# A cross-attention kernel: a new order for its first slots and its end, and output weights loaded one chunk per slot

## The chip, the cores and the metric

The kernel runs on one NeuronCore of a Trainium2 chip. The metric is the device time of one execution in microseconds (us). TensorE is written PE in the profile (its weight loads PEld), VectorE is DVE, ScalarE is ACT, GpSimd is POOL and SyncE, which issues all the DMA transfers of this kernel, is SP.

## What is computed

The input x has 32 batches of 512 rows and 640 columns; the context has 32 batches of 77 rows and 1024 columns. There are 20 heads of 32 columns. Cut to what the kernel computes (the reference also slices a further 24 context rows, but the context it is given ends after 77, so those parts are empty):

```python
q = heads(x @ to_q_w)                     # (32, 20, 512, 32)
k = heads(ctx @ to_k_w)                   # (32, 20, 77, 32)
v = heads(ctx @ to_v_w)
p = softmax(q @ k.T / sqrt(32))           # over the 77 keys
out = merge(p @ v) @ to_out_w + to_out_b + x
```

Everything is float32. To keep that precision on PE, each operand is split into a high part (a rounded copy, made by ACT) and a low part (the remainder, a subtraction on DVE or POOL), and a product is three matmuls: high by high, high by low, low by high.

## The kernel before

A first stage, up to about 284 us in the profile, turns the context into keys and values for all batches, which go to scratch memory in DRAM, splits the weights, and prepares the first batch of x. The main stage then runs 160 *slots*. Slot n works on batch b = n // 5 and on the group j = n % 5 of four heads (128 of the 640 columns). The order of the instructions on every engine is the order in which the program text emits them (the schedule is written out by hand), so each engine, SP's DMA queue included, is a queue in program order that stops at the first instruction whose inputs are not ready.

A slot holds several stages of different slots' work:

- `scores(n, t)` for the four row blocks t = 0 to 3 of slot n: three matmuls (L381) into one of three PSUM banks named sc, then a maximum on DVE (L389). `exps(n, t)` follows on ACT: four exponentials with their row sums (L399).
- `queries(n + 1, ...)`: fifteen matmuls (L346) for the next slot's queries, and `split_q(n + 1)`: three ACT copies (L357, L361) and two DVE subtractions (L363).
- `normalize(n - 1)`: reciprocal of the sums on DVE (`sums`, L409), then one large multiplication on POOL (L414). `transpose_p(n - 1)`: one DVE transpose (L421) of the normalized probabilities into the one buffer z, then four DMAs to a DRAM scratch pd (L428).
- `load_p(n - 2)`: two DMAs (L437, L438) that bring the transposed probabilities of slot n - 2 back as raw.
- for the slot three back, m = n - 3 (called *taken*, from slot 3 on): `cast_p` (ACT, L445), `rest_p` (ACT, L451, and DVE, L452), and `last_p` (POOL, L459) split raw into high and low parts pp. `values(m)` are eight matmuls (L473): the first needs only `cast_p`, the second also the subtraction of `rest_p`, and the last two also L451 and `last_p`. `split_a(m)` (L104 on ACT, L105 on DVE) splits the result into at.
- from slot 7 on, two *output pieces* of twelve matmuls each (`piece`, `project`, L503), which multiply at by the output weights wo_s for a batch that is complete; slots 0 to 6 have none (`has_out` is false). `finish` adds a finished half row block to the residual (DVE, L531) and, after the second half, sends the 128 x 640 block out (SP, L535). `load_residual` (L492) and `add_bias` (POOL, L496) prepare the residual.
- beside these, single steps for coming batches: loads of keys and values (`refill`, L323, L326, L333), of x (`load_x`, L226), and its transposes and splits (L230, L237, L238).

In slots 0 and 1, values of the last group of the context are computed as well (`context_values`, L200, 24 matmuls a call). From slot 2 on, the output weights come back from DRAM in five chunks of 640 KB (L731): two after slot 2, two after slot 3, one after slot 4.

After slot 159, `end()` drains the pipeline: it holds the probabilities of slots 157, 158 and 159, the last pieces (6 to 9) of batch 30, and all eight half row blocks of batch 31. Those are opened by `begin` with the heads that are ready and closed with the last group of heads, j = 4, after `take(N - 1)`, which is `values` and `split_a` of slot 159.

Within a slot PE's program order is: scores 0, two fifths of the queries, scores 1, the rest of the queries, scores 2, first piece, values of the slot three back, scores 3, second piece. On POOL it is: normalization of slot n - 1, low part of slot n - 3, then bias and splits. On DVE the transpose of slot n - 1 stands ahead of the query subtractions of slot n + 1.

Of the kernel before, what the change touches and what calls it, by code (L numbers as in the profile page):

```python
# [23 lines left out]
P = 128  # L24
# [26 lines left out]
def kernel(  # L51
# [25 lines left out]
    nc = tc.nc  # L77
    B, S, C = x.shape
    CA = ehs.shape[2]
    NT = B * NKEY  # L80
    NQ = S // P
    NC_ = C // P
# [3 lines left out]
    N = B * NC_  # L86
# [307 lines left out]
    def exps(n, t, sc, nm):  # L394
        if t == 0:
            sms[n] = main.tile([P, NQ * HPC], F32, tag="sm", name="sm", bufs=2)
        for i in range(HPC):
            at = t * HPC + i
            nc.scalar.activation(  # L399
                pnb[n % 2][:, at, :NKEY],  # L400
                sc[:, i * NKEY : (i + 1) * NKEY],
                AF.Exp,
                bias=nm[:, i : i + 1],
                accum_out=sms[n][:, at : at + 1],
            )

    def sums(n):
        rs = main.tile([P, NQ * HPC], F32, tag="rs", name="rs", bufs=2)
        nc.vector.reciprocal(rs, sms.pop(n))  # L409
        return rs  # L410

    def normalize(n, rs):
        pf = pnb[n % 2][:, :, :NKEY]
        nc.gpsimd.tensor_tensor(  # L414
            pf, pf, rs.unsqueeze(2).to_broadcast([P, NQ * HPC, NKEY]), ALU.mult
        )
# [31 lines left out]
    def rest_p(n):  # L448

        raw, pp = raws[n], pps[n]  # L450
        nc.scalar.copy(pp[:64, 4, :], raw[:64, 2, :])  # L451
        nc.vector.tensor_tensor(  # L452
            pp[:, 2:4, :], raw[:, 0:2, :], pp[:, 0:2, :].bitcast(F32), ALU.subtract
        )
# [62 lines left out]
    def piece(b, i):  # L517
        for t, h, j in STEPS[4 * i : 4 * i + 4]:
            if j == 0:
                output_bank(b, t, h)  # L520
            project(b, t, h, j)
            if j == NC_ - 1:
                closed.append((b, t, h))

    def finish():

        while closed:
            b, t, h = closed.pop(0)
            xr = xrs[b, t]
            cols = slice(h * HALF, (h + 1) * HALF)  # L530
            nc.vector.tensor_tensor(  # L531
                xr[:, cols], pos.pop((b, t, h))[:, :HALF], xr[:, cols], ALU.add
            )
            if h == 1:
                nc.sync.dma_start(out[b, t * P : (t + 1) * P, :], xr)  # L535

    LATE = 2
# [13 lines left out]
    def take(m):  # L551
        values(m)
        split_a(m)
# [14 lines left out]
    def slot(n, beside=()):  # L568
        b, j = divmod(n, NC_)
        ahead, more = n + 1 < N, b + 1 < B  # L570
        back, first = PIECES[j]
        bo_, has_out = b - back, b >= back
        xsplits = SPLIT_X.get(j, ((), ())) if more and n > LATE else ((), ())
        turns = TRANSPOSE_X.get(j, ((), (), ())) if more and b else ((), (), ())
        taken = takes.get(n)

        refill(b, j, 0)
        if taken is not None:
            cast_p(taken)
        s = scores(n, 0)  # L580
        if taken is not None:
            rest_p(taken)
        if n:
            normalize(n - 1, sums(n - 1))
        if taken is not None:
            last_p(taken)
        exps(n, 0, *s)
        if ahead:
            queries(n + 1, 0, 2)
        s = scores(n, 1)  # L590
        if n - LAG + 1 in pds and n > LATE:
            load_p(n - LAG + 1)
        refill(b, j, 1)
        finish()
        if j == 4 and b + 2 < B:
            load_x(b + 2, (0, 1))
        if j in RESIDUAL and b >= RESIDUAL[j][0]:
            load_residual(b - RESIDUAL[j][0], RESIDUAL[j][1])
        if j in BIAS and b >= BIAS[j][0]:
            add_bias(b - BIAS[j][0], BIAS[j][1])  # L600
        exps(n, 1, *s)
        for i in turns[0]:
            transpose_x(b + 1, i)
        if ahead:
            queries(n + 1, 2, NC_)
        s = scores(n, 2)
        if n:
            transpose_p(n - 1)
        if ahead:
            split_q(n + 1)  # L610
        exps(n, 2, *s)
        if j == 4 and b + 2 < B:
            load_x(b + 2, (2, 3))
        for c in xsplits[0]:
            split_x(b + 1, c)
        if has_out:
            piece(bo_, first)
        if taken is not None:
            values(taken)
        if len(beside) > 0:  # L620
            context_values(*beside[0], psv)
        s = scores(n, 3)
        finish()
        for i in turns[1]:
            transpose_x(b + 1, i)
        if taken is not None:
            split_a(taken)
        for c in xsplits[1]:
            split_x(b + 1, c)
        exps(n, 3, *s)  # L630
        if len(beside) > 1:
            context_values(*beside[1], psv)
        if has_out:
            piece(bo_, first + 1)
        for i in turns[2]:
            transpose_x(b + 1, i)

    def end():


        last = B - 1
        load_p(N - 2)
        cast_p(N - 3)
        rest_p(N - 3)
        last_p(N - 3)
        normalize(N - 1, sums(N - 1))
        transpose_p(N - 1)
        finish()
        add_bias(last - 1, 3)
        piece(last - 1, 6)  # L650
        piece(last - 1, 7)
        finish()
        load_p(N - 1)
        load_residual(last, 0)
        load_residual(last, 1)
        piece(last - 1, 8)
        take(N - 3)
        piece(last - 1, 9)
        cast_p(N - 2)
        rest_p(N - 2)  # L660
        last_p(N - 2)
        finish()
        spare = late[0].tile([P, 3, S], F32, tag="raw", name="xr", bufs=2)
        load_residual(last, 3, spare.rearrange("p k q -> p (k q)")[:, :C])
        load_residual(last, 2)

        def begin(i, j0, j1):
            t, h = divmod(i, 2)
            if j0 == 0:
                if i < 3:  # L670
                    pos[last, t, h] = ps.tile([P, S], F32, tag="sc", name="po", bufs=3)
                elif i == 3:
                    pos[last, t, h] = ps.tile([P, S], F32, tag="pq", name="po", bufs=1)
                elif i < 7:
                    output_bank(last, t, h)
                else:
                    pos[last, t, h] = late[1].tile([P, S], F32, tag="pa", name="po", bufs=1)
            for j in range(j0, j1):
                project(last, t, h, j)

        begin(0, 0, 2)
        begin(1, 0, 2)
        take(N - 2)
        cast_p(N - 1)
        rest_p(N - 1)
        last_p(N - 1)
        for t in (0, 1, 3, 2):
            add_bias(last, t)
        begin(2, 0, 3)
        begin(0, 2, 4)  # L690
        begin(1, 2, 4)
        begin(2, 3, 4)
        for i in range(3, 6):
            begin(i, 0, 4)
        take(N - 1)
        begin(6, 0, 4)
        begin(7, 0, 4)
        for t in range(NQ):
            for h in range(2):
                project(last, t, h, 4)  # L700
                closed.append((last, t, h))
            finish()

    with tc.manual_schedule(engines=ENGINES):
        g0, gn = GROUPS_KV[-1]
        load_keys(0, 0)
        halves = [(g0, gn, t0, h) for t0 in range(0, gn, P) for h in range(2)]
        queries(0, 0, NC_)
        split_q(0)
        for half in halves[:2]:  # L710
            context_values(*half, psv)
        for i in range(NQ):
            transpose_x(1, i)
        for c in range(2):
            split_x(1, c)
        for half in halves[2:4]:
            context_values(*half, psv)
        for n in range(LATE):
            slot(n, halves[4 + 2 * n : 6 + 2 * n])
        psv.release()  # L720
        kvp.release()
        late.append(ctx.enter_context(tc.tile_pool(name="late", bufs=1, reuse_waits="tile")))
        late.append(
            ctx.enter_context(tc.tile_pool(name="psl", bufs=1, space=PSUM, reuse_waits="tile"))
        )
        load_p(0)
        wos.append(late[0].tile([P, NC_, 2, C], FPR, name="wo_s"))
        for n in range(LATE, LATE + 4):
            slot(n)
            for k in {LATE: (0, 1), LATE + 1: (2, 3), LATE + 2: (4,)}.get(n, ()):  # L730
                nc.sync.dma_start(wos[0][:, k].bitcast(F32), wo_dram[:, k].bitcast(F32))  # L731
        for n in range(LATE + 4, N):
            slot(n)
        end()


# [38 lines left out]
```

## Time and profile before

| what | us |
|---|---|
| median of 3 runs (lowest to highest) | 1980.47 (1978.42 to 1981.48) |
| the profiled execution | 1980.38 |
| its span in the trace | 1978.6 |
| PE busy with matmuls | 1946.0 |
| ACT busy | 1595.6 |
| DVE busy | 1345.8 |
| POOL busy | 986.0 |

The profiled execution took 1980.38 us, of which the trace covers 1978.6 us from the first to the last event; the other 1.8 us lie around the traced span. "Busy" is the time in which an engine had an instruction running. For PE that does not mean full speed: the PE clock column of the profile gives the share of full speed that the hardware granted in a stretch of time, and a matmul at a lower granted clock is longer and still counts as busy. In the lists below a line gives start, duration, engine, program line, operation, output and inputs, and in brackets the idle time ahead of it with the instruction that ended it. In tables by stretch, each engine has its busy time and, in parentheses, the number of its instructions; the last three columns are the granted PE clock, the mean busy share of the 16 DMA engines and the rate in GB/s.

Most slots look alike. Slot 8, from 373.60 to 383.89 us, has PE busy for all of its 10.29 us, and so does every slot after it until 1933 us.

### The profile page before, as it was taken

The page shows a single profiled execution, that of the slowest core. Times are in us where ns is not written, and L with a number is a line of the kernel's source. Part 1 is how long each engine was busy: PE and PEld are TensorE (multiplying, and loading weights), DVE is VectorE, ACT ScalarE, POOL GpSimd, SP SyncE. Part 2 cuts the span into 40 slices and gives each one's busy share as a digit, 9 for nine tenths or more (in the row PEclk, how much of TensorE's full clock was granted, in tenths as well). Part 3 has the DMA queues.
Part 4 walks back from the last instruction along what each step waited for, and adds up shares of the span by engine and source line. Part 5 has one row for each costly group of instructions (what it writes and reads, how often), then busy time and mean ns, then how long its engine had stood idle before and what let it go on. Part 6 is the DMA issues. An engine that isn't in the chain of part 4 may idle for free.

```text
span 1978.6 us, 38192 instructions
## 1 busy us (share of the span) xinstructions
PE 1946.0 (98%) x11012; PEld 1761.7 (89%) x11012; DVE 1345.8 (68%) x2156; ACT 1595.6 (81%) x6377; POOL 986.0 (50%) x620
## 2 busy tenths in 40 slices
PE   9999998999999999999999999999999999999998
PEld 7889996799999999999999999999999999999997
DVE  4443235777777777777777777777777777777763
ACT  3322137899999999999999999999999999999982
POOL 0000033566555555565555666655665556655644
PEclk9999999899999999999999999999999999999999
DMA  7994368888889898889888988888888888888975
GB/s 170 217 263 120 96 146 206 212 220 228 228 220 229 224 225 230 225 231 225 228 223 225 226 229 221 234 223 228 226 227 226 225 224 219 225 228 225 231 195 156
DMA packets 555996, 423.54 MB, mean 214 GB/s; under 512 B 170191, under 2 KB 459501, under 8 KB 555789
## 3 DMA queue, kind: packets, MB, share of 16 engines
q1 hardware_dynamic: 555789, 421.10, 83.8%
q8 instruction: 91, 1.49, 0.3%
q14 instruction: 116, 0.95, 0.2%
HBM read 245.61 MB, written 175.32 MB: 213 GB/s over the span
## 4 chain that ended last, share of the span: by engine, by line
PE 90%; DMA 4%; SPq 2%; ACT 1%; DVE 1%; issue 1%; POOL 1%; DVEq 0%; ACTq 0%; POOLq 0%
PE po L503 28%; PE pq L346 28%; PE pa L473 15%; PE sc L381 10%; PE pv L200 4%; PE pk L171 4%; DMA raw<-pd 1%; SPq L114 1%; DMA k_dram<-ks 1%; SPq L155 1%; DMA v_dram<-vs 1%; DMA wraw<-in_L_xattn_to_k_w_dram 0%; POOL pn L414 0%; DMA wraw<-in_L_xattn_to_out_w_dram 0%; DMA cs<-in_ctx_dram 0%
## 5 line engine op out<-in xcount | busy, mean ns | idle before, releaser
L399 ACT ACTIVATE pn<-sc,nm 128x77 f32<-128x77 f32 x2560 | 797.6, 328 | 44.6 <-DVE nm L389 31.1
L414 POOL TENSOR_TENSOR pn<-pn,rs 128x1232 f32<-128x1232 f32 x160 | 364.3, 2277 | 670.2 <-DVE rs L409 655.4
L503 PE MATMUL po<-wo_s,at 128*128 128x320 f32 x3840 | 626.9, 312 | 3.0 <-DVE xr L531 3.0
L346 PE MATMUL pq<-xt,wq_s 128*128 128x512 f32 x2400 | 621.0, 399 | 0.0
L503 PEld LDWEIGHTS po<-wo_s,at 128*128 128x128 f32 x3840 | 566.3, 189 | 3.6 <-DVE xr L531 3.2
L399 ACT ACTIVATION_READ_ACCUMULATOR pn<-sc,nm 128x1 f32 x2560 | 529.3, 207 | 0.0
L389 DVE TENSOR_REDUCE nm<-sc 128x4 f32<-128x308 f32 x640 | 294.5, 460 | 335.0 <-PE sc L381 330.6
L346 PEld LDWEIGHTS pq<-xt,wq_s 128*128 128x128 f32 x2400 | 430.4, 190 | 76.7
L473 PE MATMUL pa<-pp,vb 128*128 128x512 f32 x1280 | 331.2, 400 | 13.0 <-POOL pp L459 11.0
L238 POOL TENSOR_TENSOR xt<-xs,xt 128x512 fp32r<-128x512 f32 x160 | 203.9, 1292 | 269.2 <-ACT xt L237 262.0
L473 PEld LDWEIGHTS pa<-pp,vb 128*128 128x128 f32 x1280 | 243.3, 197 | 53.7 <-POOL pp L459 13.5
L421 DVE STREAM_TRANSPOSE z<-pn 128x1280 f32<-128x1280 f32 x160 | 241.0, 1506 | 21.4 <-POOL pn L414 19.7
L452 DVE TENSOR_TENSOR pp<-raw,pp 128x1024 fp32r<-128x1024 f32 x160 | 196.2, 1226 | 59.5 <-ACT pp L445 52.8
L381 PEld LDWEIGHTS sc<-kc,qt 128*128 128x128 f32 x1280 | 213.0, 190 | 23.6 <-issue 2.1
L381 PE MATMUL sc<-kc,qt 128*128 128x154 f32 x1280 | 223.1, 256 | 2.4 <-DVE qt L363 2.3
L459 POOL TENSOR_TENSOR pp<-raw,pp 64x512 fp32r<-64x512 f32 x160 | 208.7, 1305 | 27.0 <-ACT pp L451 14.6
L363 DVE TENSOR_TENSOR qt<-pq,qt 64x512 fp32r<-64x512 f32 x320 | 214.2, 669 | 6.9 <-ACT qt L357 2.5
L496 POOL TENSOR_TENSOR xr<-xr,bias 128x640 f32<-128x640 f32 x128 | 200.8, 1570 | 9.7
L361 ACT CAST qt<-qt 64x512 fp32r<-64x512 f32 x320 | 198.1, 619 | 9.0
L381 PE MATMUL sc<-kb,qt 128*128 128x308 f32 x640 | 195.9, 306 | 0.0
L445 ACT CAST pp<-raw 128x1024 fp32r<-128x1024 f32 x160 | 170.1, 1063 | 9.3 <-DMA raw<-pd 9.2
L104 ACT CAST at<-pa 128x512 fp32r<-128x512 f32 x160 | 94.5, 591 | 94.8 <-PE pa L473 94.7
(40 smaller groups left out, 1528.5 us busy)
## 6 DMA issues: line engine op xcount, KB each, us to landing
pd<-z SPq DMA_DIRECT2D x640, 160.0 KB, 3.5
raw<-pd SPq DMA_DIRECT2D x160, 512.0 KB, 4.5
xs<-in_x_dram SPq DMA_DIRECT2D x128, 320.0 KB, 6.1
xr<-in_x_dram SPq DMA_DIRECT2D x128, 320.0 KB, 3.9
out_dram<-xr SPq DMA_DIRECT2D x128, 320.0 KB, 3.0
raw<-pd SPq DMA_DIRECT2D x160, 128.0 KB, 4.4
v_dram<-vs SPq DMA_DIRECT2D x19, 640.0 KB, 3.7
k_dram<-ks SPq DMA_DIRECT2D x80, 128.0 KB, 2.4
```

Source lines behind the costliest of these rows:

```text
L238: low.tensor_tensor(parts[1], src, parts[0].bitcast(F32), ALU.subtract)
L346: nc.tensor.matmul(pqs[n], wq_s[:, k, a, j * P : (j + 1) * P], xts[b, k][:, c, :], start=(k == 0 and m == 0), stop=(k == NC_ - 1 and m == 2),)
L363: nc.vector.tensor_tensor(qt[r, 1 + w, :], pq[r], qt[r, 0, :].bitcast(F32), ALU.subtract)
L381: nc.tensor.matmul(sc[:, cols], qt[:, m, t * P : (t + 1) * P], keys_, start=(m == 0), stop=(m == 2),)
L389: nc.vector.tensor_reduce(nm, sc[:, :KCOLS].rearrange("p (h k) -> p h k", k=NKEY), AX.X, ALU.max, negate=True)
L399: nc.scalar.activation(pnb[n % 2][:, at, :NKEY], sc[:, i * NKEY : (i + 1) * NKEY], AF.Exp, bias=nm[:, i : i + 1], accum_out=sms[n][:, at : ...
L414: nc.gpsimd.tensor_tensor(pf, pf, rs.unsqueeze(2).to_broadcast([P, NQ * HPC, NKEY]), ALU.mult)
L421: nc.vector.transpose(z.rearrange("p b t j -> p t b j"), pn.rearrange("p (t h) k -> p t (h k)", t=NQ).rearrange("p t (b i) -> p t b i", i=Q),)
L459: nc.gpsimd.tensor_tensor(pp[64:, 4, :], raw[:64, 2, :], pp[:64, 4, :].bitcast(F32), ALU.subtract)
L473: nc.tensor.matmul(pas[n], vb[:, t, :, a], pp[:, c, :], start=(m == 0), stop=(m == len(PASSES) - 1),)
L496: nc.gpsimd.tensor_tensor(xrs[b, t], xrs[b, t], bias, ALU.add)
L503: nc.tensor.matmul(pos[b, t, h][:, :HALF], ats[b * NC_ + j][:, a, t * P : (t + 1) * P], wos[0][:, j, c, h * HALF : (h + 1) * HALF], start= ...
```

## The change

- **Slots 0 to 6**, which have no output pieces: the low part on POOL (`last_p`) goes ahead of the normalization; the transpose (`transpose_p`, with its four DMAs) goes behind the query subtractions and the third group of exponentials; scores 3 go ahead of `values` and of `context_values`.
- **Slot 159**: third exponentials, first piece, scores 3, then the transpose of slot 158, fourth exponentials, second piece, and only then `take(156)`.
- **end()**: the transpose of slot 159, with its DMAs, goes behind pieces 6 and 7 of batch 30 and their additions; there is one more `finish` between those two pieces.
- **The last row blocks**: blocks 0 and 1 are closed and sent ahead of the opening of the eighth half block, not after it. The very last row block is sent in two halves of 128 x 320.
- **Output weights**: one chunk after each of slots 2 to 6.

```diff
@@ finish()
-            if h == 1:
+            if (b, t) == (B - 1, NQ - 1):
+                nc.sync.dma_start(out[b, t * P : (t + 1) * P, cols], xr[:, cols])
+            elif h == 1:
                 nc.sync.dma_start(out[b, t * P : (t + 1) * P, :], xr)
@@ slot()
         if taken is not None:
             rest_p(taken)
+        rs = sums(n - 1) if n else None
+        if taken is not None and not has_out:
+            last_p(taken)
         if n:
-            normalize(n - 1, sums(n - 1))
-        if taken is not None:
+            normalize(n - 1, rs)
+        if taken is not None and has_out:
             last_p(taken)
...
         s = scores(n, 2)
-        if n:
+        if not ahead:
+            exps(n, 2, *s)
+            piece(bo_, first)
+            s = scores(n, 3)
+        if n and has_out:
             transpose_p(n - 1)
         if ahead:
             split_q(n + 1)
-        exps(n, 2, *s)
+            exps(n, 2, *s)
+        if n and not has_out:
+            transpose_p(n - 1)
...
+        if not ahead:
+            exps(n, 3, *s)
+            finish()
+            piece(bo_, first + 1)
+            take(taken)
+            return
         if has_out:
             piece(bo_, first)
+        else:
+            s = scores(n, 3)
         if taken is not None:
             values(taken)
         if len(beside) > 0:
             context_values(*beside[0], psv)
-        s = scores(n, 3)
+        if has_out:
+            s = scores(n, 3)
         finish()
@@ end()
         normalize(N - 1, sums(N - 1))
-        transpose_p(N - 1)
-        finish()
         add_bias(last - 1, 3)
         piece(last - 1, 6)
+        finish()
         piece(last - 1, 7)
         finish()
+        transpose_p(N - 1)
         load_p(N - 1)
...
         take(N - 1)
-        begin(6, 0, 4)
-        begin(7, 0, 4)
-        for t in range(NQ):
+
+        def close(t):
             for h in range(2):
                 project(last, t, h, 4)
                 closed.append((last, t, h))
             finish()
+
+        begin(6, 0, 4)
+        close(0)
+        close(1)
+        begin(7, 0, 4)
+        close(2)
+        close(3)
@@ main stage
-        for n in range(LATE, LATE + 4):
+        for n in range(LATE, N):
             slot(n)
-            for k in {LATE: (0, 1), LATE + 1: (2, 3), LATE + 2: (4,)}.get(n, ()):
+            if n < LATE + NC_:
+                k = n - LATE
                 nc.sync.dma_start(wos[0][:, k].bitcast(F32), wo_dram[:, k].bitcast(F32))
-        for n in range(LATE + 4, N):
-            slot(n)
```

## The prediction

> **What bounds the kernel now.** I read the page first: PE is busy 98% of the span and its granted clock is 0.9 or more nearly everywhere, so PE's own work is the bound, and the change removes no matmul. It can only win where PE waits or runs slowly. The list of waits cut to stretches names two such places: slots 3 to 7 (312 to 374 us; 8.8 us of PE waiting on POOL's low part L459 there) and the end (from 1930 us; 2.0 us on L459, 3.0 us on DVE's L531). Between them PE never idles, and nothing there is edited.
>
> The table by slot, slots 3 to 8 from each slot's first score matmul:
>
> ```profile
> 312.95:325.13 12.18, 7.89 (x36) 6.22 (x36) 8.55 (x13) 11.18 (x48) 3.53 (x2) 0.97 0.91 220
> 325.13:335.76 10.63, 8.84 (x37) 7.20 (x36) 6.73 (x11) 10.40 (x42) 7.30 (x5) 0.82 0.90 242
> 335.76:348.22 12.46, 8.63 (x36) 6.73 (x36) 5.91 (x11) 8.64 (x39) 3.54 (x2) 0.91 1.11 251
> 348.22:361.46 13.24, 9.93 (x38) 7.63 (x37) 8.42 (x13) 9.42 (x40) 3.54 (x2) 0.76 0.90 198
> 361.46:373.60 12.14, 12.14 (x61) 10.86 (x61) 9.08 (x14) 11.16 (x48) 7.18 (x5) 0.84 0.84 224
> 373.60:383.89 10.29, 10.29 (x62) 9.34 (x61) 7.02 (x12) 10.15 (x42) 7.76 (x6) 1.00 0.71 183
> ```
>
> The columns after the length are PE, PEld, DVE, ACT, POOL, clock, DMA share, GB/s. The last row is the steady slot. A slot without its 24 output matmuls (two pieces of 1.80 us) should need 10.29 - 3.6 = 6.7 us of PE; it takes 10.6 to 13.2. PE waits, and also runs at a lower clock (0.76 to 0.97). But ACT is busy 8.6 to 11.2 us in each row and the DMA engines 0.90 to 1.11: with PE's waits gone, these are next. So I read ACT's timeline. It works without a break of 0.5 us from 316.4 to 335 us, and then waits twice:
>
> ```profile
> 341.01 1.05 ACT L445 CAST pp<-raw 128x1024 fp32r<-128x1024 f32 x1 [3.16 <-DMA raw<-pd]
> ...
> 353.53 1.05 ACT L445 CAST pp<-raw 128x1024 fp32r<-128x1024 f32 x1 [2.90 <-DMA raw<-pd]
> ```
>
> These are the starts of ACT's slots 5 and 6; slots 3, 4, 7 and 8 start at 317.58, 327.99, 363.43 and 373.89. The DMA answer for 327 to 333 us says why raw is late:
>
> ```profile
> wo_s<-wo_dram SPq DMA_DIRECT2D x2, 640.0 KB, 6.7
> pd<-z SPq DMA_DIRECT2D x4, 160.0 KB, 3.0
> raw<-pd SPq DMA_DIRECT2D x1, 512.0 KB, 9.3
> ```
>
> Raw takes 9.3 us to land behind two weight chunks; its median over the run is 4.5.
>
> At the end I read the timeline:
>
> ```profile
> 1935.74 0.74 PE L473 MATMUL pa<-pp,vb 128*128 128x512 f32 x2 [2.00 <-POOL pp L459]
> ...
> 1940.32 1.77 POOL L459 TENSOR_TENSOR pp<-raw,pp 64x512 fp32r<-64x512 f32 x1 [2.99 <-ACT pp L451]
> ...
> 1944.47 1.51 DVE L421 STREAM_TRANSPOSE z<-pn 128x1280 f32<-128x1280 f32 x1 [3.37 <-POOL pn L414]
> 1945.91 0.85 DVE L531 TENSOR_TENSOR xr<-po,xr 128x320 f32<-128x320 f32 x2
> ...
> 1946.42 1.17 PE L503 MATMUL po<-wo_s,at 128*128 128x320 f32 x3 [2.97 <-DVE xr L531]
> ...
> 1947.38 3.62 PE L473 MATMUL pa<-pp,vb 128*128 128x512 f32 x8
> ```
>
> DVE stands at slot 159's transpose, waiting for POOL, with the additions queued behind it that free an output bank; PE waits 2.97 us for that bank. After it, three po matmuls and eight pa take 1.17 and 3.62 us:
>
> ```profile
> 1943.44:1946.42 2.98, 0.01 (x2) 0.01 (x1) 1.95 (x3) 0.00 (x0) 2.50 (x2) 0.88 0.40 129
> 1946.42:1950.80 4.38, 4.38 (x12) 3.61 (x13) 0.34 (x1) 0.00 (x0) 0.00 (x0) 0.50 0.87 186
> ```
>
> The wait halves the granted clock for the next 4.4 us.
>
> **Slots 0 to 6, the order.** In slots 0 and 1 PE is full (12.00 of 12.00 us from 300 to 312), so scores 3 ahead of 24 context matmuls gain nothing; if they unsettled that, at most the 0.3 us of one score group would be lost. I take 0. In slot 2 the subtractions L363 come ahead of the transpose: PE's wait for them (1.89 + 0.42 us) shrinks by the transpose's 1.43, but the two maxima behind both end at 316.7 either way, and ACT goes on at 316.36 as now: 0.
>
> In slots 3 to 6 the low part no longer waits for the 2.28 us normalization. It starts when L451 ends, 1.45 us after the slot's first cast, while DVE's L452 still runs. [...] Scores 3 now stand ahead of values and wait only for a score bank, freed by ACT 2.7 us after that cast; the low part then comes in time. All 8.8 us of waiting go, and the clock loss with them. But ACT, now never short of scores, is the engine that is late next: its busy time is 9.1 us in slot 4 and 9.0 in slots 5 and 6. I give it 9.3 a slot with its short gaps.
>
> The transpose now ends 0.5 to 1.1 us later than now, and its four DMAs with it. On SP the second x load of slot 4, the weight chunk and the next key loads are queued behind them. In slot 3 that costs nothing, since SP is busy with L333 until 326.5, after the transpose's 325.1. In slot 4 x and keys follow about as early as now, because SP now spends 6.3 us on issuing the four pd DMAs into full queues.
>
> **Weights, one chunk per slot.** Each chunk is 0.655 MB, 2.65 us at the 247 GB/s that the saturated stretch carries. Before raw of slot 2 two chunks fewer are queued: 340.9 - 5.3 = 335.6. ACT's slot 5 can start at 328.0 + 9.3 = 337.3: wait gone. Before raw of slot 3 again two fewer (three sent, not five): 353.5 - 5.3 = 348.2; by issue I get 347.5 (transpose done 335.6, SP through pd, x, chunk and four key loads at 342.2, landing over 4.5 to 5.3). ACT wants it at 346.6, so a wait of 1.4 stays and slot 6 starts at 348.0. Slot 7 starts at 357.3; its raw, issued at about 351, lands near 356.3. So 363.43 becomes 357.4: **6.0 us**. Slot 7 itself is ACT-bound (10.46 us now) and passes this on to PE. Bounds: no DMA wait left, 9; raw of slot 3 not earlier than ACT's wait of slot 5 allows, or low clock in slots 6 and 7, 2.5. I stay at 6.0, the value by the landing rows. The later chunks are in time: chunk 3 issued by 348 for slot 7's first piece near 358, chunk 4 by 358 for slot 8.
>
> **Slot 159 and end().** Now after the first piece PE does six pa, waits 2.00, does two pa, scores, second piece (ends 1938.44). New: piece to 1932.15, scores to 1932.6, piece to 1934.4, eight pa to 1936.3, the low part being ready at 1935.7: 2.1 us. ACT's exponentials end about 1.7 us earlier, so low part and normalization of 157 and 159 move to 1938.6-1940.4 and 1940.4-1942.7. The additions for pieces 5 to 7 run on DVE ahead of the transpose, by 1940.6, before PE asks for the bank: the 2.97 us go. So do the slow rows: by the chain of waits 3 po, 8 pa and 24 po take 1.17 + 3.41 + 4.26 = 8.84 us, at full clock 0.45 + 1.87 + 3.60 = 5.92: 2.9 us. [...]
>
> What is late next is raw of slot 158: its load is issued at 1941.38 as now (it waits for pd, not for the edit), lands 4.1 later at 1945.5, cast and L452 to 1947.9, low part to 1949.0; PE arrives at 1947.2 and waits 0.5. So 2.1 + 3.0 + 2.9 - 0.5 = **7.5 us**. The chain of slot 159 (transpose 1942.8-1944.3, pd, raw at 1949.7, landing 1953.9, low part 1957.3) is ready 1.1 us before PE asks at 1958.4. On SP the two residual loads and an output block move with these; biases end at 1963.5, before the first closing addition. If this cover fails, each us late costs one.
>
> The closing order adds no matmul. Blocks 0 and 1 need at of slot 159, ready 1.5 us after its pa (1967.63 to 1969.13); the half block ahead of them takes 1.8. Blocks 2 and 3 still come last and DVE follows PE by 0.5 us as now. The last DMA carries 160 KB instead of 320: at 378 GB/s 0.4 less to move, against one more issue of 0.36: between -0.4 and +0.4, I take 0.
>
> **Sum.** 1980.4 - 6.0 - 7.5 = **1966.9** for the profiled execution; the median of the runs, 1980.47, is the same within 0.1.
>
> **Rivals.** *Both places, as worked out*: 1966.9, own range 1964.5 to 1969.5, chance 0.60. *DMA keeps the start*: chunks that land in slots 6 and 7 delay those slots' raw, and the start gives 2.5: 1970.4. For: DMA share 1.11 in slot 5. Against: 198 GB/s in slot 6, room for a chunk. 0.18. *No raw wait left*: start 9, 1963.9. For: raw of slot 4 took 4.2. 0.09. *The chain of slot 158 or 159 ends later than PE asks*, end 3 us short: 1969.9. For: slack of 1.1 only. 0.05. *The reorder does not help*, the waits reappearing elsewhere: 1980. Against: the bank and the POOL order are named by the rows. 0.02. [...] 0.06.
>
> **How the numbers follow.** 1966.9; range 1963.2 to 1971.5, from the no-wait case to the DMA case with its half-us errors. A measurement of this kernel can tell about 0.2% (4 us) from no change. Faster 0.92, same 0.02, slower 0.06.
>
> **What would show it.** Right: no PE wait on L459 in slots 3 to 6, L459 there 1.77 us, ACT's cast of slot 7 near 357.4, no wait on L531 near 1943, no clock under 0.9 after 1940, slot 159's pa near 1958.4. Wrong: a clock of 0.6 in slots 5 to 8, raw landing over 7 us in slot 5 or 6, or PE waiting for slot 159's low part.

## The result and the profile after

| | before | after |
|---|---|---|
| median us (runs) | 1979.45 (6) | 1972.99 (6) |
| lowest to highest | 1977.62 to 1981.48 | 1969.57 to 1975.19 |
| profiled execution, its span | 1980.38, 1978.6 | 1972.61, 1970.8 |

The ratio is 0.9965, 95% interval 0.9953 to 0.9977: faster by 0.23 to 0.47%. The prediction had the direction right and twice the size: 13.5 us forecast, 6.5 measured (1979.45 to 1972.99), and 1972.99 lies 1.5 us above its range.

The span splits at the first score matmul of slots 3, 8, 12 and 159. Times in us of the two profiled executions:

| stretch | before | after | difference | predicted |
|---|---|---|---|---|
| first event to slot 3 | 312.95 | 314.04 | +1.1 | 0 |
| slot 3 to 8 | 60.65 | 56.13 | -4.5 | -6.0 (with the next row) |
| slot 8 to 12 | 41.20 | 43.55 | +2.4 | |
| slot 12 to 159 | 1514.52 | 1515.03 | +0.5 | 0 |
| slot 159 to the end | 49.29 | 42.09 | -7.2 | -7.5 |
| sum | 1978.6 | 1970.8 | -7.8 | -13.5 |

In these two executions the end came as worked out, and where 6.0 us were forecast for the start, 4.5 were gained by slot 8 and 2.2 (4.5 - 2.4, before rounding) were left at slot 12. The same table by slot as before, slots 3 to 8 (stretch, length, PE, PEld, DVE, ACT, POOL, clock, DMA share, GB/s):

```profile
314.04:324.01 9.97, 7.55 (x36) 6.13 (x36) 6.42 (x11) 8.86 (x38) 3.42 (x2) 1.00 0.75 162
324.01:334.45 10.44, 8.26 (x36) 5.79 (x35) 6.53 (x11) 10.29 (x42) 7.78 (x6) 1.00 0.89 226
334.45:345.70 11.25, 8.64 (x36) 6.78 (x35) 7.59 (x13) 10.14 (x43) 4.63 (x3) 0.88 1.07 243
345.70:358.86 13.16, 9.31 (x36) 7.74 (x35) 8.65 (x13) 9.72 (x45) 4.01 (x2) 0.76 1.05 261
358.86:370.17 11.31, 11.17 (x60) 9.80 (x59) 9.48 (x15) 10.87 (x46) 6.24 (x4) 0.94 0.89 231
370.17:381.53 11.36, 10.84 (x62) 9.27 (x60) 7.04 (x13) 10.47 (x44) 8.20 (x7) 1.00 0.72 185
```

The POOL order did its part: PE no longer waits for L459 in slots 3 to 6. In slots 5 and 6 it waits for ACT instead, which frees the bank for the next scores:

```profile
342.18 0.41 PE L381 MATMUL sc<-kb,qt 128*128 128x308 f32 x1 [2.15 <-ACT pn L399]
...
354.60 0.62 PE L381 MATMUL sc<-kb,qt 128*128 128x308 f32 x1 [3.85 <-ACT pn L399]
```

So slot 6 (fourth row) is as long as before (13.16, was 13.24), its clock is again 0.76, and slot 8 (last row), which used to be full, now has 0.52 us without PE and takes 11.36 instead of 10.29. ACT's casts, which start its slots, say why slots 5 and 6 are long. ACT's slot 5 starts at 339.34, its slot 6 at 351.76:

```profile
339.34 1.05 ACT L445 CAST pp<-raw 128x1024 fp32r<-128x1024 f32 x1 [0.54 <-DMA raw<-pd]
...
351.76 1.04 ACT L445 CAST pp<-raw 128x1024 fp32r<-128x1024 f32 x1 [2.91 <-DMA raw<-pd]
```

The wait on raw in slot 5 shrank from 3.16 to 0.54 us. The one in slot 6 is as long as before (2.91, was 2.90). The DMA answer for 344 to 346 us has the load that it waits for, issued at 344.49:

```profile
raw<-pd SPq DMA_DIRECT2D x1, 512.0 KB, 7.2
```

It took 7.2 us to land, with three weight chunks sent instead of five; before, 7.6.

Slot 11, which the change does not edit, lost 1.3 us (11.6 instead of 10.3). The start of ACT's slot 11 before, and then after:

```profile
404.61 1.06 ACT L445 CAST pp<-raw 128x1024 fp32r<-128x1024 f32 x1
404.72 1.06 ACT L445 CAST pp<-raw 128x1024 fp32r<-128x1024 f32 x1 [1.84 <-DMA raw<-pd]
```

PE begins slot 11 at 404.48 before and at 402.12 after; the cast, which needs raw, comes at nearly the same time in both. The low part of slot 11 is then late for PE:

```profile
411.01 0.75 PE L473 MATMUL pa<-pp,vb 128*128 128x512 f32 x2 [1.01 <-POOL pp L459]
```

At the end, the rows that answer to those of before:

```profile
1938.19 1.77 POOL L459 TENSOR_TENSOR pp<-raw,pp 64x512 fp32r<-64x512 f32 x1 [1.39 <-ACT pp L451]
...
1938.88 0.82 DVE L531 TENSOR_TENSOR xr<-po,xr 128x320 f32<-128x320 f32 x2
...
1942.34 1.51 DVE L421 STREAM_TRANSPOSE z<-pn 128x1280 f32<-128x1280 f32 x1 [2.64 <-POOL pn L414]
...
1947.43 1.92 PE L473 MATMUL pa<-pp,vb 128*128 128x512 f32 x7 [0.55 <-DVE pp L452]
```

The additions now run at 1938.88, ahead of the transpose, which still waits 2.64 us for POOL, but with nothing behind it that PE needs. PE's only wait after slot 159's start is the 0.55 us for the split of slot 158's raw, predicted as 0.5, and the clock stays at 1.00 until all matmuls are done. PE asks for slot 159's pa at 1957.97, and its low part was ready at 1956.62: 1.35 us of slack, predicted as 1.1.

### The profile page after: what moved, and what is told of

Same layout as the page of the kernel before. It is cut to its first block, busy times and chain, and to the rows that moved or that the text cites. A ratio compares the mean times of both kernels' runs of the same rounds, so it can differ in the third digit from the quotient of the medians.

```text
span 1970.8 us, 38196 instructions
## 1 busy us (share of the span) xinstructions
PE 1940.5 (98%) x11012; PEld 1756.0 (89%) x11012; DVE 1347.0 (68%) x2156; ACT 1594.6 (81%) x6377; POOL 987.8 (50%) x620
## 4 chain that ended last, share of the span: by engine, by line
PE 86%; DMA 5%; ACT 2%; SPq 2%; DVE 2%; issue 1%; POOL 1%; ACTq 0%; DVEq 0%; POOLq 0%
PE po L503 27%; PE pq L346 27%; PE pa L473 14%; PE sc L381 10%; PE pv L200 4%; PE pk L171 4%; DMA raw<-pd 2%; DMA wraw<-in_L_xattn_to_out_w_dram 1%; SPq L114 1%; ACT pn L399 1%; POOL pn L414 1%; DMA wo_dram<-ws 1%; SPq L155 0%; ACT pp L445 0%; DMA cs<-in_ctx_dram 0%
## 5 line engine op out<-in xcount | busy, mean ns | idle before, releaser
L452 DVE TENSOR_TENSOR pp<-raw,pp 128x1024 fp32r<-128x1024 f32 x160 | 196.3, 1227 | 66.7 <-ACT pp L445 57.8
L459 POOL TENSOR_TENSOR pp<-raw,pp 64x512 fp32r<-64x512 f32 x160 | 210.6, 1316 | 44.8 <-ACT pp L451 32.8
```

Of the source, the lines that this page charges most:

```text
L459: nc.gpsimd.tensor_tensor(pp[64:, 4, :], raw[:64, 2, :], pp[:64, 4, :].bitcast(F32), ALU.subtract)
```

## The experiments

Each kernel was compared with executions of the kernel before from its own session (e1 to e4; e5 to e8; e9 to e12; e13 to e15), whose medians lie between 1980.19 and 1981.78 us. Across sessions, compare the ratios and not the medians. Segments are from each kernel's one profiled execution, in us; "new" and "old" say which start a kernel has. All from e9 on have the new end, e5 and e6 too.

| kernel | median | ratio to before, 95% | slot 3-8 | 8-12 | 12-159 | 159-end |
|---|---|---|---|---|---|---|
| before | | | 60.65 | 41.20 | 1514.5 | 49.29 |
| after | 1972.99 | 0.9965 (0.9953-0.9977) | 56.13 | 43.55 | 1515.0 | 42.09 |
| e1 end only | 1973.46 | 0.9970 (0.9959-0.9982) | 58.78 | 41.20 | 1514.7 | 41.76 |
| e2 start only | 1981.14 | 1.0007 (0.9997-1.0018) | 57.13 | 42.79 | 1516.9 | 46.53 |
| e3 order only | 1980.91 | 1.0004 (0.9995-1.0013) | 60.39 | 41.45 | 1516.5 | 46.54 |
| e4 chunks only | 1978.40 | 0.9997 (0.9985-1.0009) | 57.74 | 43.12 | 1517.8 | 48.06 |
| e5 new, no x of batch 2 | 1971.88 | 0.9954 (0.9941-0.9966) | 53.76 | 43.42 | 1516.0 | 41.88 |
| e6 new, chunks early | 1975.50 | 0.9977 (0.9964-0.9991) | 57.84 | 42.69 | 1517.5 | 41.98 |
| e7 transpose of end only | 1978.22 | 0.9984 (0.9971-0.9997) | 59.98 | 41.20 | 1517.2 | 44.85 |
| e8 slot 159 only | 1980.35 | 0.9997 (0.9986-1.0008) | 61.18 | 41.19 | 1514.6 | 46.49 |
| e9 new, raw first | 2184.26 | 1.1031 (1.1012-1.1050) | 59.44 | 48.02 | 1723.7 | 42.66 |
| e10 old start, raw first | 2182.73 | 1.1025 (1.1010-1.1040) | 62.46 | 43.86 | 1714.8 | 43.02 |
| e11 new, old chunks | 1972.44 | 0.9963 (0.9950-0.9977) | 59.78 | 41.65 | 1514.2 | 42.05 |
| e12 e11, raw first | 2185.85 | 1.1046 (1.1028-1.1064) | 58.99 | 46.72 | 1718.2 | 46.59 |
| e13 new, no x of batches 2, 3 | 1968.97 | 0.9941 (0.9924-0.9958) | 53.30 | 42.41 | 1514.4 | 42.00 |
| e14 new, x over two slots | 2000.10 | 1.0091 (1.0076-1.0107) | 57.93 | 41.20 | 1544.6 | 42.09 |
| e15 old start, x over two slots | 2005.71 | 1.0111 (1.0092-1.0130) | 62.96 | 41.19 | 1542.8 | 41.89 |

The old start and old chunks stand in before, e1, e7 and e8: slot 3 to 12 takes 101.9, 100.0, 101.2 and 102.4 us there. Single executions of the same code in this stretch differ by 2.4 us, which is the grain at which the segments may be read; the changed kernel's 99.7 and e2's 99.9 are hardly below the shortest of these. A profile need not be typical of its kernel's runs either: e2's is the fastest of its twelve (1977.45 of 1977.45 to 1988.10).

**The two places apart.** The edits are parts of the change's own diff, each made to the kernel before.

*e1, the end only*: the two edits shown below for e7 and e8, the order of closing and the halves of the last output:

```diff
+            if (b, t) == (B - 1, NQ - 1):
+                nc.sync.dma_start(out[b, t * P : (t + 1) * P, cols], xr[:, cols])
...
+        begin(6, 0, 4)
+        close(0)
+        close(1)
+        begin(7, 0, 4)
+        close(2)
+        close(3)
```

> Only the edits of the end (slot 159, end, closing order, halves); slots 0 to 6 and the weight chunks as before. Theory A (the end gives its 7.2 us, and the start's gain is given back because raw is bound to the absolute progress of the DMA queues): 7.2 us faster than before, 1972.2. Theory B (the start gives 4.5 us and chance took some of it): the same here, 7.2. If the end gives less than 5.5, both are wrong.

*e2, the start only*, is the edits of e3 and e4 together:

> Only the order of slots 0 to 6 and one chunk per slot; the end as before. Theory A: PE reaches slot 8 some 3 to 4.5 us earlier relative to slot 3, but PE waits for slots 8 to 12 give most of it back: 0 to 2 us faster than before, 1978.5. Theory B: 4 to 5 us faster, 1975.

*e3, of the start the order only*:

```diff
+        rs = sums(n - 1) if n else None
+        if taken is not None and not has_out:
+            last_p(taken)
         if n:
-            normalize(n - 1, sums(n - 1))
-        if taken is not None:
+            normalize(n - 1, rs)
+        if taken is not None and has_out:
             last_p(taken)
...
-        if n:
+        if n and has_out:
             transpose_p(n - 1)
...
+        if n and not has_out:
+            transpose_p(n - 1)
...
+        else:
+            s = scores(n, 3)
...
-        s = scores(n, 3)
+        if has_out:
+            s = scores(n, 3)
```

> Only the order of slots 0 to 6, chunks as before (two, two, one). Theory A: raw of slot 2 lands as late as before, so ACT's slots 5 and 6 start as before; slot 8 at most 1 us earlier, total within 1 us of before. Theory B: the order alone gives about half of 4.5, 2 us.

*e4, of the start the chunks only*:

```diff
-        for n in range(LATE, LATE + 4):
+        for n in range(LATE, N):
             slot(n)
-            for k in {LATE: (0, 1), LATE + 1: (2, 3), LATE + 2: (4,)}.get(n, ()):
+            if n < LATE + NC_:
+                k = n - LATE
                 nc.sync.dma_start(wos[0][:, k].bitcast(F32), wo_dram[:, k].bitcast(F32))
```

> Only one chunk per slot, order as before. Theory A: raw of slot 2 lands up to 2.5 us earlier, raw of slot 3 as before or later, since a chunk, a pd and an x load still stand ahead of it; slot 8 within 2 us of before, total within 2 us. Theory B: 2 us faster.

The end alone has the whole effect, 0.9970 against 0.9965 for both; the start alone has none that the runs can show, 1.0007. Theory A held in the total and in the course: with one chunk per slot (e2, e4, after) slot 3 to 8 is 56.1 to 57.7 us, against 58.8 to 61.2 with the old start and chunks (before, e1, e7, e8), and slots 8 to 12 take 42.8 to 43.6 instead of 41.2. The order alone leaves the first segment as it was (e3, 60.39). Theory B fell.

**What raw waits for.** *e5* takes four loads out (batch 2 then works on the x of batch 1, so its result is not the reference's):

```diff
-        if j == 4 and b + 2 < B:
+        if j == 4 and b == 0:
+            xss[2] = xss[1]
+        elif j == 4 and b + 2 < B:
             load_x(b + 2, (0, 1))
...
-        if j == 4 and b + 2 < B:
+        if j == 4 and b and b + 2 < B:
             load_x(b + 2, (2, 3))
```

> The changed kernel without the four loads of x for batch 2 in slot 4 (1.3 MB less; batch 2 works on what the tile still holds, so this part of the computation is left out). Theory A (raw waits behind what is queued in the DMA rings in slots 4 and 5): raw of slot 3 lands 3 us or more earlier, ACT's slot 6 starts without a wait on raw, PE goes from slot 3 to slot 8 in 53 to 54 us (56.1 in the changed kernel), slots 8 to 12 in 41.2 to 41.5 (43.6), total 4 to 5 us under the changed kernel, 1968.5. Rival C (ACT's own work and the order on POOL set slots 3 to 8): slot 3 to 8 within 0.5 us of 56.1 and the total within 1 us.

*e6* moves two chunks to where the DMA share is lower (0.53 from 300 to 313 us in the changed kernel, 0.81 from 313 to 325) and none behind slots 4 and 5:

```diff
+        for k in (0, 1):
+            nc.sync.dma_start(wos[0][:, k].bitcast(F32), wo_dram[:, k].bitcast(F32))
+        WO = {2: (2,), 3: (3,), 6: (4,)}
         for n in range(LATE, N):
             slot(n)
-            if n < LATE + NC_:
-                k = n - LATE
+            for k in WO.get(n, ()):
                 nc.sync.dma_start(wos[0][:, k].bitcast(F32), wo_dram[:, k].bitcast(F32))
```

> The changed kernel with the same five chunks at other places: two ahead of slot 2, one after slots 2 and 3, none after slots 4 and 5, one after slot 6. Theory A: about 1.3 MB go through the queues while they are half idle (share 0.5 to 0.8 up to slot 3), so raw of slots 2 and 3 lands 2 to 5 us earlier; slot 3 to 12 in 95 to 97 us (99.7), total 2 to 4 us under the changed kernel, 1970. Rival C: no difference beyond 1 us.

e5 confirmed the first half. Without the x load, slot 6's cast waits 0.78 us instead of 2.91:

```profile
349.09 1.05 ACT L445 CAST pp<-raw 128x1024 fp32r<-128x1024 f32 x1 [0.78 <-DMA raw<-pd]
```

Slot 3 to 8 takes 53.76, 2.4 us less (1.3 MB at the 243 GB/s of slot 5 would be 5.4). The second half failed: slots 8 to 12 stayed at 43.42, and the ratio went from 0.9965 to 0.9954, about 2 us and within the intervals, not 4 to 5. e6 failed: with two chunks ahead of slot 2, slot 4's cast waited 3.10 us for its raw and the next two 0.9 each, and nothing was won (0.9977). In each of the placements tried (before, after, e6), some cast waits for a raw.

**Raw at the head of the queue.** e9, e10 and e12 issue the two raw loads first in each slot, ahead of the key and value loads:

```diff
+        if n - LAG + 1 in pds and n > LATE:
+            load_p(n - LAG + 1)
         refill(b, j, 0)
...
-        if n - LAG + 1 in pds and n > LATE:
-            load_p(n - LAG + 1)
         refill(b, j, 1)
```

> The changed kernel with one more edit: the two loads of raw are issued at the head of each slot's DMA queue, ahead of the loads of keys and values. Theory A', formed from the runs so far (ACT's casts of slots 4 to 11 wait for raw, which SP issues late, behind key loads that wait for x to land, and which lands late behind x, weights and pd): raw of slots 3 and 8 is issued some 2 us earlier, slot 3 to 8 in 54.5 (56.1), slots 8 to 12 in 41.5 to 42.5 (43.6), slots 12 to 159 in 1514.3 (1515 to 1517), total 3 to 4 us under the changed kernel. Rival D (the DMA engines' bytes set it, whatever the order on SP): within 1 us of the changed kernel.

> The end of the changed kernel, order of slots 0 to 6 and chunks of the kernel before, and raw issued at the head of the queue. Theory A': slot 3 to 8 about 1 to 2 us under the 58.8 of the kernel with the end alone, slots 8 to 12 at 41.2, total 1 to 2 us under that kernel. Rival D: equal to that kernel within 1 us.

e11 is the changed kernel with e4's edit undone, and e12 is that with raw first:

> The changed kernel with the chunks as before (two, two, one). If one chunk per slot is what costs slots 8 to 12 their 2 us: slots 8 to 12 in 41.2 to 41.5, slot 3 to 8 about 60 as with the order alone, total equal to the changed kernel within 1.5 us. If the chunks do not matter: slots 8 to 12 in 43.5 here too.

> The changed kernel with the chunks as before and raw issued at the head of the queue. Theory A': slot 3 to 8 in 57 to 58, slots 8 to 12 in 41.2, total 2 us under the same kernel without the earlier issue. Rival D: no difference beyond 1 us.

e9, e10 and e12 were 10% slower, and both theories about them fell. The wait list of e9 between 375 and 1925 us, first of SP's queue and then of the engines:

```profile
SPq L437 <- DMA pd<-z: 299.0, 346, 3.1
```

```profile
DVE z L421 <- DMA pd<-z: 294.7, 115, 4.8
```

In the changed kernel the same two lines are 64.4 and 2.9 us. A raw load waits on SP until its pd has landed (the first line); at the head of the slot SP stands still for that, and the key loads and the next pd queue up behind. The next transpose needs z, which that pd has not yet read. In e9's timeline raw is issued at 991.82, eight key loads follow, pd goes out from 998.31, and the next raw at 1002.96, the next pd at 1010.06: a loop of 11.75 us through one queue, where a slot of PE's work is 10.3. In the order of before, key loads stand ahead of raw in that time. e11 shows that with the new order and the new end the old chunks do as well (0.9963): less gained up to slot 8 (59.78), less given back (41.65).

**Where the rest is given back.**

> The changed kernel without the x loads of slots 4 and 9 (batches 2 and 3 work on what the tile holds; that part of the computation is left out). Theory E (the x load of slots 4, 9, 14 ... stands ahead of the raw that the second slot after it waits for): slots 8 to 12 in 41.2 to 41.6 (43.4 with only the first load left out), ACT's tenth cast interval near 9.6 instead of 12.9. Rival F (the chunks of slots 5 and 6 push the queue back): still 43 or more.

e13 extends e5's edit to batch 3 (`b < 2` and `xss[b + 2]` for `b == 0` and `xss[2]`, `b > 1` for `b`). ACT's interval that begins with its slot 10 is 10.28 us (12.92 in e5, 12.75 in the changed kernel), and the cast of slot 11 no longer waits for raw:

```profile
400.29 1.06 ACT L445 CAST pp<-raw 128x1024 fp32r<-128x1024 f32 x1
```

So the second x load, in slot 9, is what held slot 11's raw: theory E. Slots 8 to 12 fell only from 43.42 to 42.41, half of what it said. The remaining 1.2 us are all in slot 8 (11.50 us; the three after it take 10.28 to 10.32), where PE, ahead of ACT, waits 0.63 us for an output bank and loses the rest in gaps too short for the list. In the changed kernel it is much the same: PE begins slot 8 at 370.17, 1.8 us ahead of ACT's cast at 371.98 (before: 0.3), and loses 1.07 of that in the slot. Of the 1.8 us, 0.77 are a wait of that cast for its raw, which left behind the fifth chunk.

> The changed kernel with the second half of each x load one slot later (slots 0 of a batch instead of 4), and the first of the four transposes one slot later with it. Theory E: raw of slots 3 and 8 lands 1 to 2.6 us earlier; slot 3 to 8 in 54 to 55 (56.1), slots 8 to 12 in 41.5 to 42.5 (43.6), fewer stalls later, 1 to 4 us under the changed kernel. Rival F: within 1 us of it. Against both: the later half may now collide with the transposes and cost something in every fifth slot, up to 30 times 0.5 us.

> The end of the changed kernel, slots 0 to 6 and chunks as before, and the second half of each x load one slot later. Theory E: raw of slot 3 lands earlier here too; slot 3 to 8 about 1 us under 58.8, the total 0 to 2 us under the kernel with the end alone.

```diff
-    TRANSPOSE_X = {0: ((), (0,), ()), 1: ((1,), (2,), ()), 2: ((3,), (), ())}
+    TRANSPOSE_X = {1: ((0, 1), (2,), ()), 2: ((3,), (), ())}
...
-        if j == 4 and b + 2 < B:
-            load_x(b + 2, (2, 3))
+        if j == 0 and b and b + 1 < B:
+            load_x(b + 1, (2, 3))
```

e14 makes this edit in the changed kernel, e15 in the kernel with the new end alone. In e14 slots 8 to 12 came down to 41.20, neither slot 6's nor slot 11's cast waits for raw, and ACT's interval from slot 5 to 6 is 9.41 us instead of 12.42: the mechanism of E again. But the first transposes of x then stand on DVE ahead of their data, once per batch, the case "against both" of the expectation, and the first such stall already puts slot 3 to 8 at 57.93, not the 54 to 55 expected (e15: 62.96, not under 58.8). The wait list of e14:

```profile
DVE xs L230 <- DMA xs<-in_x_dram: 60.8, 20, 7.0
...
DVE xs L230 <- DMA vb<-v_dram: 32.3, 11, 4.8
```

Slot 12 to 159 takes 30 us more. No version that computes everything beats the changed kernel by more than the intervals, e11 included.

**The end, part by part.**

e7 moves the transpose alone, e8 changes slot 159 alone, both in the kernel before:

```diff
-        transpose_p(N - 1)
-        finish()
         add_bias(last - 1, 3)
         piece(last - 1, 6)
+        finish()
         piece(last - 1, 7)
         finish()
+        transpose_p(N - 1)
```

> The kernel before with one edit: in the end, the transpose of slot 159 behind pieces 6 and 7 and their additions, with the extra addition step between them. Both theories: the 2.97 us wait for the bank goes and with it the halved clock (2.9 us), less about 0.5 us of waiting for slot 158's raw: 5.4 us faster, 1975. If the clock did not follow from the wait: 2.5 us.

```diff
         s = scores(n, 2)
+        if not ahead:
+            exps(n, 2, *s)
+            piece(bo_, first)
+            s = scores(n, 3)
...
+        if not ahead:
+            exps(n, 3, *s)
+            finish()
+            piece(bo_, first + 1)
+            take(taken)
+            return
```

> The kernel before with one edit: the order of slot 159. The 2.0 us wait on the low part of slot 156 goes, and the normalization of slot 159 comes about 1.7 us earlier, but PE still waits for the bank behind the transpose: 1.5 to 2.1 us faster, 1978.7. [...]

In e7 the wait for the bank is gone and slot 159 to the end is 44.85, 4.4 us less (5.4 expected): the 3.0 us wait and its 2.9 us of lower clock went, but 3.4 us at half clock now follow the 2.00 us wait on L459 ahead of it, where 48 matmuls take 8.78 us instead of some 7.2. In e8 it is 46.49, 2.8 less: the wait for the bank is longer, 3.46 us, since PE arrives sooner, but only 3.4 us of half clock follow, where before had 6.8. The two together with the closing order give 7.5 (e1); no run has the closing order alone. The interval of the whole runs of e8 includes no difference.

The old end also appears in e2, e3 and e4, with the same edits as in before, and takes 46.5, 46.5 and 48.1 us there against 49.3 in before. In e2 the wait for the bank is as long as in before, and the matmuls behind it run at full speed (clock 1.00 from 1946 to 1950 us):

```profile
1946.22 0.71 PE L503 MATMUL po<-wo_s,at 128*128 128x320 f32 x3 [2.98 <-DVE xr L531]
...
1946.77 2.02 PE L473 MATMUL pa<-pp,vb 128*128 128x512 f32 x8
```

In before the wait was 2.97 and the same two groups took 1.17 and 3.62 us. In e3 the 3.4 us of half clock come ahead of the wait, which is 1.5 us shorter for it; in e4 they come behind it, for 3.4 us instead of 6.8.

## Why the prediction was half right

**The end was right**, term by term: no wait for L459 in slot 159, the additions ahead of the transpose, the 0.5 us for slot 158's raw, slot 159's chain ready 1.35 us early. One term holds for the execution that was read and not for every other: the 2.9 us of lower clock. In three other executions of the same end it was smaller or absent (total 46.5 to 48.1 us, not 49.3), so "the wait halves the granted clock" is not a rule. The profiles' 7.2 us come so near to 7.5 also because they are measured against the very execution that was read; against e2's old end the same new end is 4.4 us shorter (46.53 to 42.09). The runs put the end alone at 0.30% (0.18 to 0.41%, 3.6 to 8.1 us), which is 5.9 us and does not exclude 7.5.

**The start was wrong at the step "Weights, one chunk per slot"**, in two terms.

First, "340.9 - 5.3" and "353.5 - 5.3" credit every byte not yet queued to the raw behind it, at the full rate of 247 GB/s. That could hold only if the queues stayed full. They did not: the DMA share is 0.75 in slot 3 of the changed kernel, 0.91 before. And in slots 4 and 5 pd, 1.3 MB of x and one chunk still leave SP shortly ahead of slot 3's raw, as before. It landed after 7.2 us, where the estimate had 4.5 to 5.3, and was issued at 344.49, where it had 342.2 (343.3 with slot 3's later start). Counted from the start of slot 3 it landed 2.9 us earlier than before, not 5.3. That the x load is what it stood behind is shown by e5; that the gap in slot 3 is where the missing bytes went is argued from the shares. The prediction had given 2.5 us as its lower bound for the start, and its own sign of being wrong, "raw landing over 7 us in slot 5 or 6", came true. The measured start of ACT's slot 7 is 42.3 us after its slot 3 (45.9 before); predicted 39.8. Of the 2.5 us between, 2.05 are waits on raw (0.54 and 2.91 where 1.4 was allowed), the rest ACT's own work, some 9.5 us a slot where 9.3 was taken.

Second, "passes this on to PE" took the gain at slot 7 as final. Raw of slot 8 stands behind the x load of slot 9 (e13), in absolute time nearly where it was: issued at 398.39 and cast at 404.61 before, at 398.98 and 404.72 after, although PE was 2.4 us ahead at slot 11. At slot 12 PE was 1.1 us ahead; it had lost 1.07 us at slot 8 as well. In all ten kernels that leave both x loads and raw at their places (before, after, e1 to e4, e6 to e8, e11), this raw lands 90.2 to 92.5 us after slot 3 begins, whatever the start looks like; without the two x loads (e13) it lands after 84.4. Before, it was issued at 398.39, took 5.65 us to land, and was cast 0.57 us later without a wait: just in time, so the small slack could have been read in the profile before. The prediction looked at raw in the slots that the change edits, not in those that it moves.

Of the rivals, "DMA keeps the start" (2.5 us, 0.18) comes nearest: raw did keep the start, but behind the x loads more than behind the chunks that it names, and its 1970.4 is still 2.6 us under the measured median. No run shows the course behind the chance of 0.06 for slower: the lower clock did come back in slots 5 and 6 of the changed kernel (0.88, 0.76), after waits on ACT of 2.15 and 3.85 us, but PE still began slot 8 1.8 us ahead of ACT's cast, so up to there ACT and its raw set the pace and not PE's clock.

**The low part beside L452** took nearly as long as the forecast has it, 1.77 us by the row at 1940.32, where POOL's L459 starts during DVE's L452 (1939.71 to 1940.93): it takes 1.73 to 1.76 us in slots 3 to 6 of the changed kernel, where it also starts during L452, and 1.26 to 1.27 before, where it starts after it. What makes it longer no run tests. It cost nothing there: PE has no wait for L459 in these slots.

**Left open.** Slot 3 begins 1.1 us later in the changed kernel, in code that nothing edits; over all kernels it begins between 312.3 and 317.3, so one execution says nothing about it. Slot 12 to 159 takes 1514.2 to 1517.8 us (e9, e10, e12, e14 and e15 apart) where 147 slots of the median 10.30 us come to 1514.1; whether the new start makes such waits more frequent can't be told from one profile for each kernel. So where the 2.2 us left at slot 12 go in the runs stays open; what the runs show is that the start edits as a whole change the time by -0.03% to +0.18% (e2).

## What to carry to other kernels

A gain in the first slots of a long pipeline is only kept if every later link has slack for it: look up the next transfers that arrive "just in time" in the stretch that is merely moved, not only in the edited one. Don't credit bytes taken out ahead of a transfer with their full time before you know that the queue stays full in between (here 5.3 us were credited and 2.9 came). And for an instruction that waits at the head of an in-order queue (a transpose on DVE, a load on SP), ask what stands behind it: moving the waiting transpose back, behind work that was ready, took 4.4 us off the end in e7's profile; moving the waiting raw load forward, ahead of other loads, cost over 200 us in e9.

## What the runs showed of the hardware

In the changed kernel, the table of two stretches around slot 5's wait:

```profile
339.70:343.10 3.40, 1.25 (x8) 1.05 (x8) 2.10 (x4) 3.35 (x17) 1.99 (x2) 1.00 0.96 258
343.10:346.50 3.40, 3.40 (x11) 2.78 (x10) 2.42 (x3) 3.32 (x15) 2.02 (x1) 0.50 1.12 255
```

PE is idle for 2.15 of 3.40 us at clock 1.00, and the next 3.40 us have a clock of 0.50. Waits of one length were not always followed by a lower clock: behind before's 2.97 us at the end the clock is 0.50 for 6.8 us, behind e2's 2.98 us it is 1.00 from 1946 to 1950 us; behind e4's wait for the same bank, 3.0 us, 3.4 us of half clock follow. What decides between these was not shown. So the same wait can cost 2.9 us of clock, as worked out from before's rows, or nothing, and the clock read in one execution is a number of that execution.
